# Sparse attention layer on one core: the rows of q tiles 10 and 11 go over DRAM into quarter order and are turned by VectorE instead of TensorE; two W_v transfers are issued later

## The chip, the cores and the metric

The kernel runs on one core of a Trainium2 chip. A core has five engines with a queue each: TensorE (PE; its weight loads are shown apart as PEld), VectorE (DVE), ScalarE (ACT), GpSimd (POOL) and SyncE (SP, which only issues transfers). ACT and POOL issue transfers too; all of them share 16 DMA engines. The metric is the device time of one execution in microseconds (us), the median of several runs; lower is better.

## The reference

x is 2708 x 1024, adj a random 0/1 matrix of 2708 x 2708 with about 4 ones in a row.

```
h = max(layernorm(x), 0)
q = h @ W_q.T + b_q ;  k = h @ W_k.T + b_k ;  v = h @ W_v.T + b_v
z = (q @ k.T) / sqrt(1024) * adj ;  z = -10000 where z == 0
out = x + relu(softmax(z, axis=1) @ v)
```

Everything is fp32.

## The kernel before, in words

**The mathematics.** Only the few pairs (row, neighbour) with adj = 1 count. The kernel forms M = W_q.T W_k once, then q' = h M + b for each row, and a score is the product of a row of q' with the neighbour's row of h. The weighted sum u of neighbours' rows of h comes before the product with W_v. So there are two long matrix products: "q units", rows of h times M, and "o units", rows of u times W_v.

**Tiles and units.** Rows are put in an order by number of neighbours (first 8 tiles of 128 rows, `EARLY = 8`, then the others). A unit is a pair of tiles and does a 256 x 1024 by 1024 x 1024 product by Strassen's scheme with seven block products instead of eight. Units 0 to 9 are q units on tiles (0,1) to (18,19), units 10 to 18 are o units; a single tile of u comes at the end. Unit 5 holds tiles 10 and 11. `FIRST = 4` is the first unit whose rows are read along with the attention, `last_q = 9`.

**One unit on TensorE** (`multiply`, L1050, and `opened`, L1016): `opened(n)` does a11 M11 into bank X, copies X to bank Y (L1024, ACT), then s1 T0 into bank Z, and copies Z to p5 (L1029, ACT). `multiply(n)` then does s2 T1 into Y, copies Y to u2 (L1060), a12 M into X, s4 M into Z, s3 T2 into Y, then `between(n)`, which opens the next unit, and a22 T3 into Y. The calls `after(0)` to `after(6)` between these blocks hang everything else on places "(n, i)": the operands of the next unit, loads, steps of the attention. s1 to s4 are sums of the quarter blocks a11, a12, a21, a22 of the unit's rows, transposed.

**The transposes.** The product needs the rows with the 1024 columns on the partitions. `half_turned` (L410 to L416) does this on TensorE, four 128 x 128 transposes into a PSUM bank, and ACT copies the bank to SBUF (L718), or VectorE reads it (L722). A unit of two tiles needs 16 transposes. For most tiles of u another way is in use: ACT copies the 128 x 1024 tile with its 32-column pieces regrouped (L944), writes it to DRAM (L946), four transfers from SP (`by_quarters`, L695 to L701) read it back with groups of 32 rows and of 256 columns exchanged, and VectorE turns the 32 x 32 blocks (`faces`, L703, two instructions of 128 x 512 for a tile). `is_faced` (L708) tells `blocks` (L711), which way a row tile came.

**The rows of q units.** Tiles 0 to 7 are kept from the normalisation. From unit 4 on, GpSimd gathers rows of h (L612, `load_rows`, L1204) by a table in row order. At place (2, 5) GpSimd's hand-written order is: add tiles 8 and 9 to the sum of all rows `hsum` (`owe`, L291, four adds of 128 x 256 for a tile, L298), gather the rows of unit 4, add tiles 10, 6 and 7, gather the rows of unit 5. Row tiles share 7 buffers (`ROWS = 7`).

**The order of work.** Until unit 3 ACT and DVE follow the order of the program text; from unit 4 on only DVE does, and a planner places the instructions of the other engines by its own times. `tc.issue_after(i)` puts an instruction behind i on i's engine.

**Attention** (`attention`, L959): VectorE multiplies and sums rows gathered by GpSimd (L610) with q rows (L863, scores) and then sums them with weights (L923). `advance` doles out these steps in the places. They start at the end of unit 4, once the table of the first 8 tiles is read back on SP (`reload`, L634, L638; step "b0" at place (4, 4)) and the q rows of a tile are gathered. An o unit's rows must be finished by then; the last single tile is turned by one VectorE instruction into `T_alone` (L1334).

**W_v.** In the q units the buffer M holds W_q.T W_k. Its block M[0][1], called t1 here, is free once the derived blocks T are made; in the o units it must hold W_v's block (0,1) minus block (0,0). At place (7, 0) SP loads block (0,0) into it (L1274, 1 MB), ACT negates it in two pieces (L1280), and GpSimd issues a transfer that adds block (0,1) (L1281, place (7, 6)). It is first used at place (9, 3), by VectorE (L1285). GpSimd, SP and ACT run ahead of the places where nothing holds them.

Of the kernel before, what the change touches and what calls it, by code (L numbers as in the profile page):

```python
# [10 lines left out]
FT = mybir.dt.float32  # L11
# [54 lines left out]
def tile_preln_masked_attention(  # L66
# [45 lines left out]
    q_late = dram.tile([(BARE - EARLY) * P, D], FT, name="q_late")  # L112
    u_dram = dram.tile([FULL * P, D], FT, name="u_dram")
# [195 lines left out]
    def follow(steps):  # L309

        for step in steps.split():
# [15 lines left out]
            elif step[0] == "p":  # L327
                counted(first)
            elif step[0] == "c":
                counts(*halves[first])  # L330
            elif step[0] == "o":
                sorted_at.append(sort(*halves[first]))
            elif step[0] == "w":
                pooled.close()
                with tc.issue_after((behind if first < EARLY else products)[-1].ins):
                    entered.append(put(first, int(last[0]) + 1))
            elif step == "z":
                pooled.enter_context(tc.manual_schedule(engines={mybir.EngineType.Pool}))
                with tc.issue_after(entered[-1].ins):
                    reload(EARLY, NT)  # L340
            elif step[0] == "b":
                reload(*halves[first])
            elif step[0] == "g":
                squared(first)
            else:
                if step[0] == "e":
                    counted(first)
                if step[0] != "j":
                    found(first, *[range(int(o[0]), int(o[-1]) + 1) for o in only])
                if step[0] != "i":  # L350
                    listed(first)
# [343 lines left out]
    def by_quarters(dst, rows):  # L695

        faced.append(dst)
        for a in range(QUADS):
            cols = slice(a * D // QUADS, (a + 1) * D // QUADS)
            nc.sync.dma_start(dst[a * QP:(a + 1) * QP, :].rearrange("r (g j) -> r g j", g=QUADS),  # L700
                              rows[:, cols].rearrange("(g r) j -> r g j", r=QP))  # L701
# [61 lines left out]
    def natural_rows(n):  # L763
# [252 lines left out]
    def opened(n):  # L1016
# [15 lines left out]
    def between(n):  # L1032
# [3 lines left out]
        else:  # L1036
            opened(n + 1)
        if n == last_q - 1:
# [11 lines left out]
    def multiply(n, results, after):  # L1050
# [9 lines left out]
        nc.scalar.copy(u2, Y)  # L1060
# [23 lines left out]
    def q_results(ta, tb):  # L1084
# [136 lines left out]

    products = []
# [14 lines left out]
    for n, unit in enumerate(units):  # L1237
# [8 lines left out]
        if n in (last_q, last_q + 1):  # L1246
            share -= 2.3 / 7 * (n - last_q + 1)
        nxt = units[n + 1] if n + 1 < len(units) else None
# [4 lines left out]
        def after(i):  # L1253
# [18 lines left out]
            for at, place, src in (((-2, 0), t1, of_wv(0, 0)), ((0, 3), b21, of_wv(1, 0))):  # L1272
                if (n - last_q, i) == at:
                    nc.sync.dma_start(place, src)  # L1274
# [3 lines left out]
            if (n - last_q, i) == (-2, 6):  # L1278
                for h in range(2):
                    nc.scalar.activation(t1[:, 2 * h:2 * h + 2], t1[:, 2 * h:2 * h + 2], AF.Copy, scale=-1.0)  # L1280
                nc.gpsimd.dma_start(t1, of_wv(0, 1), accum_op=ALU.add)  # L1281
# [18 lines left out]
            elif (n, i) == (FIRST, 6):  # L1300
                advance(share)
# [21 lines left out]
            if (n, i) == (3, 4):  # L1323
                searched()
            if (n, i) == (3, 6):
# [254 lines left out]
```

## Time and profile before

| | us |
|---|---|
| median of 3 runs | 629.07 |
| the runs | 627.19, 629.07, 629.32 |
| the profiled execution's own time | 627.16 |
| its span, first to last instruction | 625.5 |

The profiled execution has 6068 instructions in its span. In the chain of waits of the profile one unit's seven block products are 56 matmul records; times in the timeline are microseconds from the start of the span. The place (n, i) of the code is not in the profile; it is found from the order of the block products: the rows of unit 5 are transposed at 216.94 and 221.24 us, and the last o unit ends near 609 us. In a row of a timeline the brackets at the end tell how long the engine had been idle before it and what released it. A row of a source line gives durations in ns as least/median/greatest.

### The profile page before, as it was taken

The page shows a single profiled execution, that of the slowest core. Times are in us where ns is not written, and L with a number is a line of the kernel's source. Part 1 is how long each engine was busy: PE and PEld are TensorE (multiplying, and loading weights), DVE is VectorE, ACT ScalarE, POOL GpSimd, SP SyncE. Part 2 cuts the span into 40 slices and gives each one's busy share as a digit, 9 for nine tenths or more (in the row PEclk, how much of TensorE's full clock was granted, in tenths as well). Part 3 has the DMA queues.
Part 4 walks back from the last instruction along what each step waited for, and adds up shares of the span by engine and source line. Part 5 has one row for each costly group of instructions (what it writes and reads, how often), then busy time and mean ns, then how long its engine had stood idle before and what let it go on. Part 6 is the DMA issues. An engine that isn't in the chain of part 4 may idle for free.

```text
span 625.5 us, 6068 instructions
## 1 busy us (share of the span) xinstructions
PE 618.3 (99%) x1571; PEld 309.9 (50%) x1571; DVE 525.7 (84%) x1024; ACT 291.0 (47%) x421; POOL 368.9 (59%) x394
## 2 busy tenths in 40 slices
PE   9999999999999999999999999999999999999996
PEld 5777776444444444454444444444444444444442
DVE  5999878987988947979898999998988899898541
ACT  3538976749777373434331532443442433432300
POOL 2638870786668577856655343577577657752331
PEclk9999999999999999999999999999999999999998
DMA  8998898687797559997696999999999999995571
GB/s 336 407 374 318 332 352 326 211 273 292 267 370 277 175 180 364 342 347 233 218 362 170 397 340 313 339 326 320 328 328 320 333 306 338 288 301 144 137 266 71
DMA packets 65808, 183.24 MB, mean 293 GB/s; under 512 B 10039, under 2 KB 20615, under 8 KB 65128
## 3 DMA queue, kind: packets, MB, share of 16 engines
q0 software_dynamic: 26656, 86.02, 43.7%
q1 hardware_dynamic: 32170, 72.06, 33.0%
q10 hardware_dynamic: 6942, 24.73, 10.1%
q8 instruction: 14, 0.23, 0.1%
q14 instruction: 26, 0.21, 0.1%
HBM read 147.23 MB, written 43.88 MB: 306 GB/s over the span
## 4 chain that ended last, share of the span: by engine, by line
PE 90%; DMA 3%; POOL 2%; ACT 2%; DVE 1%; issue 0%; POOLq 0%; ACTq 0%
PE ps L1011 42%; PE psy L1011 30%; PE ps_y L476 7%; PE ps_x L476 4%; PE ps_z L476 4%; PE pt L415 2%; POOL hsum L298 2%; DMA x<-in_x_dram 2%; ACT sized L368 1%; DMA wlow<-in_wq_dram 1%; DVE wlow L444 1%; DVE s L722 0%; ACT junk_x L246 0%; PE ps_h L1230 0%; PE ps_v L594 0%
## 5 line engine op out<-in xcount | busy, mean ns | idle before, releaser
L610 POOL DMA_INDIRECT g<-h_dram,tab x93 | 120.5, 1296 | 62.4 <-issue 19.4
L1011 PE MATMUL psy<-wlow,s 128*128 128x512 f32 x320 | 144.0, 593 | 0.2 <-ACT u L1060 0.2
L1011 PE MATMUL ps<-M,a 128*128 128x512 f32 x320 | 144.1, 593 | 0.1
L863 DVE SCALAR_TENSOR_TENSOR junk<-g,pq 128x1024 uint8<-128x1024 f32 x92 | 112.3, 1220 | 9.3 <-DMA g<-h_dram,tab 7.3
L1011 PE MATMUL ps<-M,s 128*128 128x512 f32 x240 | 107.9, 592 | 0.0
L1011 PEld LDWEIGHTS ps<-M,a 128*128 128x128 f32 x320 | 60.0, 190 | 72.6 <-issue 71.5
L1011 PEld LDWEIGHTS psy<-wlow,s 128*128 128x128 f32 x320 | 60.0, 190 | 72.5 <-issue 71.3
L923 DVE SCALAR_TENSOR_TENSOR u<-g,coef,u 128x1024 f32<-128x1024 f32 x70 | 89.8, 1282 | 7.2 <-ACT u L912 5.4
L389 DVE FIND_INDEX8 at<-ones,adj 128x8 uint32<-128x685 f32 (+1 forms) x88 | 74.4, 863 | 0.0
L1011 PEld LDWEIGHTS ps<-M,s 128*128 128x128 f32 x240 | 45.5, 190 | 57.2 <-issue 55.5
L1011 PE MATMUL psy<-wlow,a 128*128 128x512 f32 x160 | 71.9, 592 | 0.0
L368 ACT ACTIVATE sized<-adj 128x2708 uint8<-128x2708 f32 (+1 forms) x22 | 54.3, 2468 | 7.5 <-DMA adj<-in_adj_dram 6.2
L298 POOL TENSOR_TENSOR hsum<-hsum,x 128x256 f32<-128x256 f32 (+1 forms) x56 | 38.6, 725 | 24.9 <-DVE wlow L444 21.5
L1115 POOL DMA_INDIRECT y<-in_x_dram,tab x19 | 33.2, 1749 | 31.4 <-ACT y L1132 16.6
L1011 PEld LDWEIGHTS psy<-wlow,a 128*128 128x128 f32 x160 | 30.4, 190 | 38.3 <-issue 36.6
L808 POOL DMA_INDIRECT out_dram<-y,tab x21 | 27.9, 1329 | 15.8 <-issue 13.6
L1011 PE MATMUL ps<-wlow,s 128*128 128x512 f32 x80 | 36.0, 593 | 0.0
L944 ACT COPY v<-u 128x1024 f32<-128x1024 f32 x20 | 20.9, 1046 | 29.9 <-DVE u L923 27.6
L912 ACT ACTIVATE u<-g,coef 128x1024 f32<-128x1024 f32 x16 | 18.4, 1148 | 25.7 <-DVE coef L911 20.5
L626 POOL DMA_INDIRECT tab_dram<-tab,pos_i x22 | 21.6, 982 | 14.3 <-DVE pos_i L689 8.8
L276 ACT ACTIVATE x<-x,r 128x1024 f32<-128x1024 f32 (+1 forms) x22 | 25.9, 1235 | 6.9 <-POOL r L266 6.9
L760 ACT COPY ps<-bp_sb 128x512 f32<-128x512 f32 x42 | 24.6, 596 | 8.7 <-DVE y L1150 7.2
(253 smaller groups left out, 839.1 us busy)
## 6 DMA issues: line engine op xcount, KB each, us to landing
adj<-in_adj_dram SPq DMA_DIRECT2D x21, 1354.0 KB, 11.4
x<-in_x_dram SPq DMA_DIRECT2D x21, 512.0 KB, 7.7
h_dram<-x ACTq DMA_DIRECT2D x21, 512.0 KB, 7.9
u_dram<-v ACTq DMA_DIRECT2D x20, 512.0 KB, 8.2
or<-u_dram SPq DMA_DIRECT2D x80, 128.0 KB, 7.9
q_late<-q SPq DMA_DIRECT2D x12, 512.0 KB, 8.5
pq<-q_late POOLq DMA_DIRECT2D x12, 512.0 KB, 9.3
M<-in_wv_dram SPq DMA_DIRECT2D x3, 1024.0 KB
```

The costliest lines, as they stand in the source:

```text
L276: nc.scalar.activation(xs[i][:n], xs[i][:n], AF.Relu, bias=r[:n, 4, i:i + 1], scale=r[:n, 3, i:i + 1])
L298: small.append(nc.gpsimd.tensor_add(hsum[:n, cols], hsum[:n, cols], xt[:n, cols]))
L368: nc.scalar.activation(sized[:n], a[:n, :, :PW], AF.Abs, accum_out=total[:n, t:t + 1])
L389: nc.vector.max_index(at[:n, k - first_k, g, :], ones[:n, 0:8], a[:n, g, :])
L476: mm = nc.tensor.matmul(bank, a_tile(o + H * a[0], a[1], i), b(o), start=first and o == 0, stop=(o == H - 1), skip_group_check=True)
L610: return nc.gpsimd.indirect_dma_start(out=dst, out_offset=None, in_=src, in_offset=off, bounds_check=N - 1, oob_is_err=False)
L760: nc.scalar.copy(return_[h], row[:, h * NB:(h + 1) * NB])
L808: to = nc.gpsimd.indirect_dma_start(out=out, out_offset=bass.IndirectOffsetOnAxis(ap=ptab.bitcast(U32)[:n, t, SLOTS:SLOTS + 1], axis=0), i ...
L863: chained(lambda: nc.vector.scalar_tensor_tensor(junk, g_of[t][s], 1.0, tq[t], op0=ALU.mult, op1=ALU.mult, accum_out=zall[:, t, s:s + 1]))
L923: chained(lambda: nc.vector.scalar_tensor_tensor(u, g_of[t][s], coef[:, s:s + 1], u, op0=ALU.mult, op1=ALU.add))
L1011: mm = nc.tensor.matmul(bank, a[:, c, :], b[:, c, :], start=False, stop=(c == 3), skip_group_check=True)
L1115: return nc.gpsimd.indirect_dma_start(out=y[:n], out_offset=None, in_=x, in_offset=off, compute_op=ALU.add)
```

## The change

The rows of unit 5 (tiles 10 and 11) take the way that tiles of u take. Once unit 4 is opened, ACT copies each of the two gathered tiles with its columns regrouped and writes it to a new DRAM buffer (`send_round`); SP reads each back with four transfers (`come_round`); VectorE turns them, two instructions of 128 x 512 a tile, at place (4, 2), where both halves are now made. For that the gather of tiles 10 and 11 stands ahead of the adds of tiles 10, 6 and 7 to `hsum`, and the gather of unit 6's rows is called at place (3, 4). The table's read back "b0" moves from (4, 4) to (4, 0), behind the transfers of `come_round` on SP, and the store of q tile 8 stands behind it.

Block (0,0) of W_v is loaded at (7, 5), behind the newest store of q on SP, and the store of q tile 16 stands behind that load. The negation on ACT and the adding transfer on GpSimd move to (8, 1), behind the newest u2 copy and the newest gather of the attention.

```diff
@@ by_quarters takes the queue and returns its last transfer
-    def by_quarters(dst, rows):
+    def by_quarters(dst, rows, eng=nc.sync):
...
             elif step[0] == "b":
-                reload(*halves[first])
+                with tc.issue_after(came[-1].ins):
+                    tabbed.append(reload(*halves[first]))
...
-                (3, 1): "i21", (3, 3): "p21", (3, 4): "j21 c0", (3, 5): "g0", (3, 6): "w0-7 g1 g2 g3 g4", (4, 4): "b0"}
+                (3, 1): "i21", (3, 3): "p21", (3, 4): "j21 c0", (3, 5): "g0", (3, 6): "w0-7 g1 g2 g3 g4", (4, 0): "b0"}
...
         if n == FIRST:
             follow("o0")
+            send_round(ROUND[0])
...
+        if n == FIRST - 1:
+            come_round(ROUND[0], nc.sync)
...
-            (nc.scalar if t < 4 else nc.sync).dma_start(dst, q)
+            behind_it = early_wv if t == units[last_q - 1][1] else tabbed if t == EARLY else None
+            with tc.issue_after(behind_it[-1].ins) if behind_it else nullcontext():
+                stored.append((nc.scalar if t < 4 else nc.sync).dma_start(dst, q))
...
+    ROUND = range(FIRST + 1, FIRST + 1 + 1)
+    stored, copied_at, came, tabbed, early_wv = [], [], [], [], []
+
+    def in_quarters(v, u):
+        return nc.scalar.copy(v.rearrange("p (a c r) -> p c a r", a=QUADS, r=QP),
+                              u.rearrange("p (c a r) -> p c a r", a=QUADS, r=QP))
+
+    def round_row(n, k):
+        t = 2 * (n - ROUND[0]) + k
+        return r_dram[t * P:(t + 1) * P, :]
+
+    def send_round(n):
+
+        for k, xt in enumerate(rows_of[n]):
+            v = row_tile(f"way_{n}_{k}")
+            in_quarters(v, xt)
+            nc.scalar.dma_start(round_row(n, k), v)
+
+    def come_round(n, eng):
+
+        rows_of[n] = [row_tile(f"came_{n}_{k}") for k in range(2)]
+        for k, xt in enumerate(rows_of[n]):
+            came.append(by_quarters(xt, round_row(n, k), eng))
...
                 rows_of[FIRST] = load_rows(units[FIRST])
+                rows_of[FIRST + 1] = load_rows(units[FIRST + 1])
                 owe(10)
                 owe(6)
                 owe(7)
-                rows_of[FIRST + 1] = load_rows(units[FIRST + 1])
...
-            for at, place, src in (((-2, 0), t1, of_wv(0, 0)), ((0, 3), b21, of_wv(1, 0))):
-                if (n - last_q, i) == at:
-                    nc.sync.dma_start(place, src)
+            if (n - last_q, i) == (-2, 5):
+                with tc.issue_after(stored[-1].ins):
+                    early_wv.append(nc.sync.dma_start(t1, of_wv(0, 0)))
+            if (n - last_q, i) == (0, 3):
+                nc.sync.dma_start(b21, of_wv(1, 0))
...
-            if (n - last_q, i) == (-2, 6):
-                for h in range(2):
-                    nc.scalar.activation(t1[:, 2 * h:2 * h + 2], t1[:, 2 * h:2 * h + 2], AF.Copy, scale=-1.0)
-                nc.gpsimd.dma_start(t1, of_wv(0, 1), accum_op=ALU.add)
+            if (n - last_q, i) == (-1, 1):
+                with tc.issue_after(copied_at[-1].ins), tc.issue_after(gathered[-1].ins):
+                    for h in range(2):
+                        nc.scalar.activation(t1[:, 2 * h:2 * h + 2], t1[:, 2 * h:2 * h + 2], AF.Copy, scale=-1.0)
+                    nc.gpsimd.dma_start(t1, of_wv(0, 1), accum_op=ALU.add)
...
-                    with tc.issue_after(products[-1].ins) if n + 1 == FIRST else nullcontext():
+                    if n + 1 != ROUND[0]:
+                        with tc.issue_after(products[-1].ins) if n + 1 == FIRST else nullcontext():
+                            ops_of[n + 1][1]()
+                if i == (4 if n == 0 else 5 if turn else 2):
+                    if n + 1 == ROUND[0]:
                         ops_of[n + 1][1]()
-                if i == (4 if n == 0 else 5 if turn else 2):
                     ops_of[n + 1][2]()
...
                 searched()
+                rows_of[FIRST + 2] = load_rows(units[FIRST + 2])
```

More of the change, by code (lines that the diff above doesn't have):

```diff
@@ L699, in by_quarters @@
             cols = slice(a * D // QUADS, (a + 1) * D // QUADS)
-            nc.sync.dma_start(dst[a * QP:(a + 1) * QP, :].rearrange("r (g j) -> r g j", g=QUADS),
-                              rows[:, cols].rearrange("(g r) j -> r g j", r=QP))
+            last = eng.dma_start(dst[a * QP:(a + 1) * QP, :].rearrange("r (g j) -> r g j", g=QUADS),
+                                 rows[:, cols].rearrange("(g r) j -> r g j", r=QP))
+        return last
     def faces(dst, xt, lo, hi):
@@ L1059, in multiply @@
         u2 = small("u2")
-        nc.scalar.copy(u2, Y)
+        copied_at.append(nc.scalar.copy(u2, Y))
         after(2)
@@ L1247, in tile_preln_masked_attention @@
             share -= 2.3 / 7 * (n - last_q + 1)
+        if n > FIRST and n + 1 in ROUND:
+            share -= 0 / 7
         nxt = units[n + 1] if n + 1 < len(units) else None
@@ L1300, in after @@
             elif (n, i) == (FIRST, 6):
-                advance(share)
+                advance(1 * share)
             if nxt is not None:
```

1 line of the change is left out of this document (added).

## The prediction

> **What bounds the kernel now.** First the page, busy shares and the DMA slices; then TensorE's own waits; then the chain of waits in order of time.
>
> ```profile
> PE 618.3 (99%) x1571; PEld 309.9 (50%) x1571; DVE 525.7 (84%) x1024; ACT 291.0 (47%) x421; POOL 368.9 (59%) x394
> ```
> ```profile
> DMA  8998898687797559997696999999999999995571
> ```
> ```profile
> PE ps_y L511 <- POOL hsum L121: 1.2, 1, 1.2
> PE ps_x L476 <- DMA wlow<-in_wq_dram: 0.2, 1, 0.2
> PE psy L1011 <- ACT u L1060: 0.2, 1, 0.2
> ```
> ```profile
> 216.94 0.87 PE pt L415 x8
> 217.81 3.44 PE psy L1011 x8
> 221.24 0.87 PE pt L415 x8
> ```
>
> TensorE is busy 99% of the span, and all its waits together are 1.6 us, 1.4 of them before its products begin. In the chain, eight matmul records of 512 columns take 3.44 us, eight transposes 0.87 us, and one piece begins where the last ended. So a cut in TensorE's work shows in full as long as nothing else comes late, and between its first and last product nothing outside TensorE can give more than those waits. The two transposing pieces at 216.94 and 221.24 are the rows of tiles 10 and 11. The change takes them away.
>
> ```profile
> L415 PE MATMUL pt<-ident,qr 128*128 128x128 f32 x96 | 12.4, 273 | 0.0
> ```
>
> **What is removed.** Of these 96 the 16 of one unit, 2 x 0.87 = 1.74 us of TensorE, and three ACT copies out of PSUM. This is the whole gain; every other edit can only cost.
>
> A page weighs this otherwise. The Trainium skill, page "VectorE: DVE Perf Modes", section "The three transpose paths", gives 390 ns for one 128 x 128 transpose on TensorE (bf16), and its rules advise TensorE for it where PSUM will do. Its figure would make the gain 16 x 0.39 = 6.2 us, an estimate from that page; its advice speaks against the move. In this trace a pipelined transpose takes 0.87/8 = 0.11 us, so I keep 1.74.
>
> **The way over DRAM: is it in time?** Unit 5's first product sets the clock:
>
> ```profile
> 232.42 6.87 PE ps L1011 x16
> ```
>
> After the change it stands at 232.42 - 1.74 = 230.7: a11 is due then, s1 3.4 us later, at 234.1. The rows in the order in which they are used: ACT's timeline, the lines of the copy, of the reading back and of the turns (least/median/greatest, ns), the DMA issues (KB, us to landing), VectorE's timeline, and the windows (PE, PEld, DVE, ACT, POOL busy, clock, DMA share, GB/s).
>
> ```profile
> 209.93 0.57 ACT L1024 COPY psy<-ps 128x512 f32<-128x512 f32 x1 [1.06 <-PE ps L1011]
> 213.54 0.58 ACT L1029 COPY p<-ps 128x512 f32<-128x512 f32 x1 [3.04 <-PE ps L1011]
> ```
> ```profile
> L944 ACT COPY v<-u x20: 1044/1046/1050, 249.1 to 586.5; 128x1024 f32<-128x1024 f32 x20
> ```
> ```profile
> L700 SPq DMA_DIRECT2D or<-u_dram x80: 302/431/1187, 321.2 to 592.3; - x80
> ...
> DMA to landing us min/median/max: 3.1/7.9/15.6
> ```
> ```profile
> L705 DVE STREAM_TRANSPOSE a<-or x29: 660/704/708, 347.3 to 573.6; 128x512 f32<-128x512 f32 x29
> ```
> ```profile
> u_dram<-v ACTq DMA_DIRECT2D x20, 512.0 KB, 8.2
> ```
> ```profile
> q_dram<-q SPq DMA_DIRECT2D x4, 512.0 KB, 3.7
> ```
> ```profile
> 221.43 0.91 DVE L1270 MEMSET g<- 128x1024 f32 x1 [0.16 <-issue]
> ```
> ```profile
> 229.03 0.69 DVE L1100 TENSOR_TENSOR q<-ps,u 128x512 f32<-128x512 f32 x1 [2.67 <-PE ps L1011]
> ```
> ```profile
> 200.00:216.00 16.00, 16.00 (x52) 7.92 (x52) 13.46 (x40) 6.86 (x11) 9.07 (x12) 1.00 0.48 166
> 216.00:226.00 10.00, 10.00 (x37) 5.36 (x36) 7.70 (x10) 9.03 (x17) 8.17 (x16) 1.00 0.19 61
> 226.00:240.00 14.00, 14.00 (x34) 6.11 (x34) 3.59 (x8) 5.31 (x10) 10.25 (x14) 1.00 0.93 319
> 300.00:310.00 10.00, 10.00 (x24) 4.37 (x23) 9.37 (x13) 3.37 (x6) 6.22 (x4) 1.00 0.61 205
> 310.00:335.00 25.00, 25.00 (x72) 11.95 (x71) 21.33 (x33) 8.24 (x15) 10.31 (x9) 1.00 0.79 269
> ```
>
> (1) ACT: the regrouping copies stand between the copies at 209.93 and 213.54, where ACT was idle 3.04 us. 210.5 + 2 x 1.05 = 212.6: 0.9 us are left, and the copies cost nothing; without that gap they would push the copy p, which is not needed for another 10 us (s4's product follows s2's and a12's). (2) The two stores, issued at 211.6 and 212.6, land after 3.7 us (the q stores, in calmer time) to 8.2 us (the same store later, under full DMA): at 215.3 and 216.3, or at 219.8 and 220.8. (3) SP issues eight transfers at 0.43 us: the last four from 217.0 to 218.7, or from 221.5 to 223.2. They land 3.1 to 7.9 us later, so the second tile is there between 221.8 and 231.1. I take the early end: DMA was at 0.48 and 0.19 of its time here, against 0.93 in the next stretch. (4) VectorE is at its memsets until 221.43 + 0.91 = 222.3; then four turns of 0.70 and four sums of 0.69, as long as the add at 229.03, make 5.6 us. By the early end a11 is ready at 223.0 and the last sum at 227.9, beside the add's 229.03 - 1.74 = 227.3, which no product waits for at once. By the late end the first tile's rows land at 229.4: a11 at 230.1 and a12 at 230.8; then a22 and a21 until 232.5 and s1 at 233.2. That is still in time, by 0.6 us for a11 and 0.9 us for s1. So TensorE loses nothing by either end; only the worst landing of that line, 15.6 us, brings a stall (rival D).
>
> What queues behind: on SP the store of q tile 7 and the table's read back, in GpSimd's queue three tiles of hsum behind two gathers.
>
> ```profile
> 225.16 0.38 SPq L638 DMA_DIRECT2D tab<-tab_dram  x1
> ```
>
> The read back waits for the table's writes and was issued at 225.16; the eight transfers are issued by 223.2 at the latest, so it loses nothing. The GpSimd work is the same in sum; I give it 0.
>
> Against the turns stands a rule of the Trainium skill, page "SBUF — State Buffer", section "SBUF: two separate sides": while VectorE holds the port pair that it shares with GpSimd, GpSimd can't write the descriptors of its transfers. The page doesn't say whether a turn holds that pair; what it would do here is rival C.
>
> **The W_v transfers.** The load in its old place on SP, the wait for it on ACT, the adding transfer, and on VectorE the add before the store that the load is now behind, the first score, and the line of t1's first use:
>
> ```profile
> 226.28 0.52 SPq L1274 DMA_DIRECT2D M<-in_wv_dram  x1
> ```
> ```profile
> 231.71 2.00 ACT L1280 ACTIVATE M<-M 128x1024 f32<-128x1024 f32 x2 [3.45 <-DMA M<-in_wv_dram]
> ```
> ```profile
> M<-in_wv_dram POOLq DMA_DIRECT2D x1, 1024.0 KB, 12.0
> ```
> ```profile
> 308.86 0.68 DVE L1100 TENSOR_TENSOR q<-ps,u 128x512 f32<-128x512 f32 x1
> ```
> ```profile
> 238.31 1.23 DVE L863 SCALAR_TENSOR_TENSOR junk<-g,pq 128x1024 uint8<-128x1024 f32 x1 [3.18 <-DMA g<-h_dram,tab]
> ```
> ```profile
> L1285 DVE TENSOR_TENSOR wlow<-wlow,M x2: 2283/2284/2284, 359.0 to 371.3; 128x2048 f32<-128x2048 f32 x2
> ```
>
> The load goes from 226.28 to behind the store of q tile 14, whose add ended at 308.86 + 0.68 = 309.5: issue near 309.5 - 1.7 = 308. It took 231.71 - 226.28 = 5.4 us; 12.0 is the row of the adding transfer. So it lands at 313 to 320, ACT negates for 2.0, and the adding transfer ends at 327 to 334. It is due at 359.0 - 1.7: over 20 us spare, no cost. On the DMA engines 2 MB move into 308 to 335. At 269/0.79 = 340 GB/s they take 6.2 us, and the two later windows have 0.39 x 10 + 0.21 x 25 = 9 us free: it fits. In its old place the load's 1 MB took 3.3 us at 319 GB/s, ahead of the first gathers. The first score, which waited for its gather until 238.31, can begin up to 3.3 us earlier; this gives VectorE slack, not TensorE time. At the new place ACT waits for the load with copies for TensorE behind it, and GpSimd for the negation with gathers behind it. I take 0 for both, for the old place cost TensorE nothing either, and carry the ends to the rivals.
>
> **The sum.** The profiled execution took 627.16 us (span 625.5). 627.16 - 1.74 + 0 = 625.4, a factor of 0.9972. That execution stands at the low end of the runs; against their median of 629.07 the forecast is 629.07 x 0.9972 = 627.3 us.
>
> **The rivals.**
>
> *A, the last tile takes the gain back.*
>
> ```profile
> 598.20 1.25 DVE L705 STREAM_TRANSPOSE T_alone<-or 128x1024 f32<-128x1024 f32 x1 [10.62 <-DMA or<-u_dram]
> ```
> ```profile
> 602.52 3.43 PE ps L1011 x8
> ```
>
> T_alone is ready at 599.45, after 10.62 us of waiting for its rows; TensorE uses it at 602.52, after the change at 600.8. That leaves 1.3 us. If VectorE's attention ends later by more than that, each microsecond is paid in full, and 3.0 us leave the time where it is: 627.2, median 629.1. For it: VectorE is 21.33 of 25 us busy in the last window above, and GpSimd's wait for the negation (0 to 7 us, by the landing) holds up gathers. Against it: the attention begins up to 3.3 us earlier, and the transfers fit.
>
> *B, slower: ACT stands before the negation.*
>
> ```profile
> 313.25 0.57 ACT L1024 COPY psy<-ps 128x512 f32<-128x512 f32 x1 [1.59 <-PE ps L1011]
> ```
> ```profile
> 320.95 3.44 PE psy L1011 x8
> ```
>
> If the planner puts the two negations ahead of the copy psy of unit 8 (313.25, after the change 311.5), ACT waits there for the 1 MB. TensorE needs that copy at 320.95 - 1.74 = 319.2. The load must land by 319.2 - 0.6 - 2.0 = 316.6, 8.6 us after its issue; from there each microsecond is one of TensorE. By the 12.0 us row it is 3.4 us: 627.16 - 1.74 + 3.4 = 628.8, median 630.7. For it: ACT did wait 3.45 us for this load. Against it: the load took 5.4 us there, at a DMA share of 0.93.
>
> *C, GpSimd is locked out by the turns.* Four turns, 2.8 us, hold up the table's writes and so the first gathers; with A's 1.3 us TensorE would lose 1.5 at the end: 626.9, median 628.8. Against it:
>
> ```profile
> 347.31 1.29 DVE L705 STREAM_TRANSPOSE a<-or 128x512 f32<-128x512 f32 x2
> ```
> ```profile
> 347.41 0.99 POOL L610 DMA_INDIRECT g<-h_dram,tab  x1 [0.30 <-DVE junk L863]
> ```
>
> A gather issued amid two turns took 0.99 us and did not wait for their end at 348.6. By that rule, if it covers turns, it would have; the trace disagrees.
>
> *D, the rows of unit 5 land late.* With 15.6 us from 223.2 they are there at 238.8 and s1 at 240.9, 6.8 us late: 632.2, median 634.1. Against it: the idle DMA of that stretch. That the rows stay on TensorE, the change doing nothing, would be 629.1; the diff marks them as faced, so I give it next to nothing.
>
> **How the numbers follow.** Chances: forecast 0.70, A 0.12, B 0.07, C 0.03, D 0.03, and 0.05 for a little more than 1.74, as the 0.2 us wait of mid-kernel and a shorter end could add (2.3: median 626.8). The runs stand in two groups 2 us apart (627.19, and 629.07 with 629.32), so the median after may be one of the lower group: 627.19 x 0.9972 = 625.4. Half a per cent, about what a measurement of this kernel can tell from no change, is 3.1 us: the bounds are 625.9 and 632.2. Faster needs the forecast or more (0.75) and the lower group (0.27): 0.20. Slower needs D, or B beyond its 12.0 us: 0.07. Within: 0.73. The range goes from 624.9 (lower group, 0.5 us more gained) to 630.6 (B), which leaves out D and a gain of over 2.3.
>
> **What would show it.** Right: 80 instead of 96 transposes pt<-ident,qr; unit 5 opened near 230.7; four turns on VectorE from 222.3; PE's waits still under 2 us; the last product 1.7 us earlier. Wrong: a wait of PE on ACT between 311 and 320 (B), on VectorE near 600 (A) or 230 (D), or writes of the table over 1 us long beside the turns (C). The forecast is wrong if PE's waits grow by over a microsecond, or if the planner reorders ACT or SP elsewhere so that a bank comes late.

## The result, and the profile after

The changed kernel takes 633.04 us (median of seven runs, 631.37 to 636.86), the kernel before beside it 627.6 us: ratio 1.0083, 95% interval 1.0059 to 1.0107. It is slower by 5.4 us, and the forecast of 627.3 us and its range up to 630.6 us both missed. The profiled execution took 633.04 us (span 631.3).

The half of the change that goes over DRAM ran nearly to the time forecast. These are timelines of the kernel after (start, duration, instruction): ACT's copies and stores, SP's reading back, VectorE's turns; then the chain of waits.

```profile
210.55 1.05 ACT L1234 COPY way<-qr 128x1024 f32<-128x1024 f32 x1
211.63 0.33 ACTq L1246 DMA_DIRECT2D r_dram<-way  x1
```
```profile
214.55 3.88 SPq L702 DMA_DIRECT2D came<-r_dram  x8
```
```profile
221.94 1.83 DVE L708 STREAM_TRANSPOSE a<-came 128x512 f32<-128x512 f32 x3
223.70 0.67 DVE L708 STREAM_TRANSPOSE s<-came 128x512 f32<-128x512 f32 x1
```
```profile
213.64 6.87 PE psy L1014 x16
220.50 6.87 PE ps L1014 x16
...
230.81 6.87 PE ps L1014 x16
```

The transposes of unit 5 are gone from the chain, and the unit opens at 230.81 instead of 232.42. So TensorE was 1.6 us ahead. It was lost, and more, in TensorE's own waits, which stand a good 120 us later: the groups of PE's waits, and its timeline (in brackets the idle time before a product, and what ended it).

```profile
PE psy L1014 <- DVE q L1105: 3.0, 1, 3.0
PE ps_y L513 <- POOL hsum L122: 1.2, 1, 1.2
PE ps L1014 <- DVE s L745: 1.0, 1, 1.0
PE psy L1014 <- ACT u L1066: 0.6, 1, 0.6
```
```profile
352.66 3.60 PE L1014 MATMUL ps<-M,s 128*128 128x512 f32 x8
...
356.91 3.70 PE L1014 MATMUL psy<-wlow,s 128*128 128x512 f32 x8 [0.65 <-ACT u L1066]
361.63 3.67 PE L1014 MATMUL ps<-M,a 128*128 128x512 f32 x8 [1.02 <-DVE s L745]
365.14 3.60 PE L1014 MATMUL ps<-M,s 128*128 128x512 f32 x8
371.73 5.40 PE L1014 MATMUL psy<-wlow,a 128*128 128x512 f32 x8 [2.99 <-DVE q L1105]
376.96 3.60 PE L1014 MATMUL psy<-wlow,s 128*128 128x512 f32 x8
```

Between the starts at 352.66 and 376.96 lie five products. Without waits they take 5 x 3.43 = 17.2 us; here they took 24.3. So 7.1 us were lost within 25 us: 1.6 gained, 7.1 lost, 5.5 net. The three waits are 4.7 us of it. Another 1.8 us are in the product at 371.73, which took 5.40 us instead of 3.60 although the profile names no wait inside it: TensorE's granted clock fell to 0.50 right behind the longest stall (windows: length, busy time of PE, PEld, DVE, ACT and POOL, clock, DMA share, GB/s).

```profile
372.00:373.00 1.00, 1.00 (x3) 0.25 (x3) 1.00 (x3) 0.15 (x2) 0.00 (x0) 0.70 1.01 275
373.00:374.00 1.00, 1.00 (x3) 0.48 (x2) 1.00 (x1) 0.53 (x2) 0.00 (x0) 0.50 1.12 277
```

So part of the loss is not a wait, but comes behind one. The waits name three different releasers, so the reader must look for what stands behind all three. Most of it stands one step back, on ACT and on VectorE:

```profile
354.71 0.59 ACT L763 COPY ps<-bp_sb 128x512 f32<-128x512 f32 x1 [7.59 <-DMA bp_sb<-in_bv_dram]
355.24 1.14 ACT L906 ACTIVATE u<-hsum,m 128x1024 f32<-128x1024 f32 x1
356.29 0.57 ACT L1066 COPY u<-psy 128x512 f32<-128x512 f32 x1
```
```profile
354.66 0.69 DVE L1387 TENSOR_TENSOR bp_sb<-bp_sb 128x512 f32<-128x512 f32 x1 [6.10 <-DMA bp_sb<-in_bv_dram]
```
```profile
338.46 0.35 SPq L1385 DMA_DIRECT2D bp_sb<-in_bv_dram  x1
```

Both engines stand still for the row of v's bias, 512 KB issued at 338.46; VectorE goes on 16.2 us later. Behind the bank's copy on ACT queues u2's copy, for which TensorE waits first; behind the subtraction on VectorE queue the rows of the next unit and the sums q. Before the change the same row came in 10.5 us, and ACT waited 0.76 us:

```profile
340.24 0.38 SPq L1344 DMA_DIRECT2D bp_sb<-in_bv_dram  x1
```
```profile
350.79 0.59 ACT L760 COPY ps<-bp_sb 128x512 f32<-128x512 f32 x1 [0.76 <-DMA bp_sb<-in_bv_dram]
```
```profile
bp_sb<-in_bv_dram SPq DMA_DIRECT2D x1, 512.0 KB, 10.5
```

The row itself was not touched by the change. What did change is the work of the DMA engines in front of it. The windows (PE, PEld, DVE, ACT, POOL busy, clock, DMA share, GB/s), before and after:

```profile
320.00:330.00 10.00, 10.00 (x37) 5.41 (x36) 9.79 (x18) 4.30 (x8) 2.29 (x2) 1.00 0.94 305
330.00:335.00 5.00, 5.00 (x13) 2.13 (x13) 3.37 (x10) 1.61 (x3) 0.57 (x1) 1.00 0.19 40
335.00:340.00 5.00, 5.00 (x13) 2.25 (x12) 4.96 (x6) 0.81 (x2) 4.37 (x3) 1.00 0.65 209
340.00:345.00 5.00, 5.00 (x13) 2.25 (x12) 4.86 (x5) 1.16 (x2) 3.78 (x5) 1.00 1.01 282
```
```profile
320.00:330.00 10.00, 10.00 (x31) 4.90 (x30) 9.11 (x19) 5.78 (x12) 3.79 (x4) 1.00 0.98 281
330.00:335.00 5.00, 5.00 (x13) 2.20 (x12) 3.98 (x4) 1.29 (x2) 3.62 (x2) 1.00 1.08 198
335.00:340.00 5.00, 5.00 (x13) 2.28 (x12) 4.70 (x5) 0.57 (x1) 3.85 (x4) 1.00 1.03 321
```

Before, the DMA engines had worked off their backlog by 330, and there was a pause ahead of the row's issue at 340.24, with shares of 0.19 and 0.65. After, there is no pause: they go into the row's time full. The suspect is the late pair of W_v transfers, which the experiments test:

```profile
306.67 1.67 SPq L1308 DMA_DIRECT2D M<-in_wv_dram  x1
```
```profile
317.97 2.00 ACT L1317 ACTIVATE M<-M 128x1024 f32<-128x1024 f32 x2 [5.77 <-DMA M<-in_wv_dram]
```
```profile
320.28 0.99 POOL L1318 DMA_DIRECT2D M<-in_wv_dram  x1 [4.63 <-ACT M L1317]
```

A second transfer behind the row came late as well: the load of W_v's block (0,0) into M[0][0], the operand of the first product of unit 10, which starts at 361.63.

```profile
344.29 0.33 SPq L1046 DMA_DIRECT2D M<-in_wv_dram  x1
```

It landed 17.2 us after its issue, at 361.5. Without any stall its product would have stood at 352.66 + 2 x 3.43 = 359.5, 2 us earlier. In this execution VectorE's s ended at the same moment and is the releaser named.

### The profile page after: what moved, and what is told of

Its sections match the earlier page's. It is cut to its first block, busy times and chain, and to the rows that moved or that the text cites. A ratio compares the mean times of both kernels' runs of the same rounds, so it can differ in the third digit from the quotient of the medians.

```text
span 631.3 us, 6055 instructions
## 1 busy us (share of the span) xinstructions
PE 619.6 (98%) x1555; PEld 308.7 (49%) x1555; DVE 528.0 (84%) x1028; ACT 292.9 (46%) x420; POOL 370.0 (59%) x394
## 3 DMA queue, kind: packets, MB, share of 16 engines
q10 hardware_dynamic: 7230, 25.78, 10.5%
## 4 chain that ended last, share of the span: by engine, by line
PE 86%; DMA 9%; DVE 2%; issue 1%; ACT 1%; POOL 0%; SPq 0%; POOLq 0%; DVEq 0%; ACTq 0%
PE ps L1014 39%; PE psy L1014 28%; PE ps_y L478 7%; PE ps_x L478 4%; PE ps_z L478 4%; DMA or<-u_dram 3%; DMA bp_sb<-in_bv_dram 3%; DMA g<-h_dram,tab 2%; PE pt L417 2%; DMA M<-in_wv_dram 2%; PE ps_y L513 1%; DVE u L926 1%; DVE s L725 0%; DVE junk L866 0%; ACT M L1317 0%
## 5 line engine op out<-in xcount | busy, mean ns | idle before, releaser
L612 POOL DMA_INDIRECT g<-h_dram,tab x93 | 121.8, 1310 | 69.1 <-DVE u L926 30.5
L1014 PE MATMUL psy<-wlow,a 128*128 128x512 f32 x160 | 73.7, 604 | 3.0 <-DVE q L1105 3.0
L1123 POOL DMA_INDIRECT y<-in_x_dram,tab x19 | 33.4, 1757 | 32.8 <-ACT y L1140 18.3
L478 PE MATMUL ps_y<-wlow 128*128 128x512 f32 x64 | 27.6, 592 | 0.0
```

Source lines behind the costliest of these rows:

```text
L478: mm = nc.tensor.matmul(bank, a_tile(o + H * a[0], a[1], i), b(o), start=first and o == 0, stop=(o == H - 1), skip_group_check=True)
L612: return nc.gpsimd.indirect_dma_start(out=dst, out_offset=None, in_=src, in_offset=off, bounds_check=N - 1, oob_is_err=False)
L1014: mm = nc.tensor.matmul(bank, a[:, c, :], b[:, c, :], start=False, stop=(c == 3), skip_group_check=True)
L1123: return nc.gpsimd.indirect_dma_start(out=y[:n], out_offset=None, in_=x, in_offset=off, compute_op=ALU.add)
```

## The experiments

Kernels of one group ran on one chip beside the kernel before. Ratios are to that kernel.

| group | kernel | median us | before us | ratio | 95% interval |
|---|---|---|---|---|---|
| I | round_only | 626.2 | 627.55 | 0.9982 | 0.9969 to 0.9996 |
| I | wv_only | 632.18 | 627.55 | 1.0078 | 1.0054 to 1.0102 |
| I | no_wv | 626.62 | 627.55 | 0.9977 | 0.9964 to 0.9991 |
| I | no_add | 625.01 | 627.55 | 0.9958 | 0.9943 to 0.9972 |
| II | after_bias_act | 633.61 | 630.86 | 1.005 | 1.0027 to 1.0073 |
| II | round_bias_act | 631.73 | 630.86 | 1.002 | 1.0 to 1.004 |
| II | add_late | 631.87 | 630.86 | 1.0033 | 1.0008 to 1.0058 |
| II | plain | 635.74 | 630.86 | 1.0083 | 1.0057 to 1.0109 |
| III | mid_wv | 628.07 | 627.46 | 1.0007 | 0.9994 to 1.0019 |
| III | after_again | 631.87 | 627.46 | 1.0076 | 1.0058 to 1.0095 |
| III | plain_again | 627.54 | 627.46 | 1.0 | 0.9976 to 1.0024 |
| III | round_only_again | 626.51 | 627.46 | 0.9984 | 0.9968 to 1.0 |
| IV | no_bias | 628.31 | 627.32 | 1.0016 | 1.0001 to 1.0031 |
| IV | dummy | 629.49 | 627.32 | 1.0034 | 1.0014 to 1.0055 |
| IV | after_third | 632.26 | 627.32 | 1.0074 | 1.0053 to 1.0094 |
| IV | plain_third | 629.73 | 627.32 | 1.0038 | 1.0011 to 1.0064 |

**Group I: each half alone, and the two transfers left out.** The kernel round_only undoes the W_v edits (its code, shortened):

```
-            if (n - last_q, i) == (-2, 5):
-                with tc.issue_after(stored[-1].ins):
-                    early_wv.append(nc.sync.dma_start(t1, of_wv(0, 0)))
...
+            for at, place, src in (((-2, 0), t1, of_wv(0, 0)), ((0, 3), b21, of_wv(1, 0))):
+                if (n - last_q, i) == at:
+                    nc.sync.dma_start(place, src)
...
+            if (n - last_q, i) == (-2, 6):
...
+                nc.gpsimd.dma_start(t1, of_wv(0, 1), accum_op=ALU.add)
```

> The changed kernel with the W_v edits undone: block (0,0) of W_v is loaded, negated and added to at the places of before; the way of tiles 10 and 11 over DRAM stays. Theory W (the late W_v transfers fill the DMA engines ahead of the load of the bias row, L1385 of the changed kernel; its landing went from 10.5 to 16.2 us and ACT and VectorE waited 7.6 and 6.1 us for it): the stall between 354 and 372 us is gone, ACT waits under 1 us for the bias row, ratio to before 0.997 (627.6 - 1.75 = 625.9). Theory R (the way over DRAM itself, by its order or its transfers): still slow, ratio 1.005 to 1.010. Theory E (the attention begins earlier because the load is not in front of its first gathers, and its gathers now meet the bias row): fast as well, since the load is back in front.

The other half, wv_only, puts the two late transfers into the kernel before.

> The kernel before with the W_v edits alone: the load behind the store of q tile 14, the negation and the adding transfer at (8, 1); q rows 10 and 11 are turned by TensorE as before. Theory W: slow, by the 6.6 us of stalls of the changed kernel without its gain of 1.75: ratio 1.007 to 1.012, ACT waits 5 us or more for the bias row. Theory E: slow in the same way, since the attention begins earlier here too. Theory R: no change, 0.998 to 1.002.

Two kernels take work out of the changed kernel: no_wv the load, the negation and the adding transfer of the block, no_add the adding transfer alone (the line that it leaves out):

```
-                    nc.gpsimd.dma_start(t1, of_wv(0, 1), accum_op=ALU.add)
```

> The changed kernel without the three W_v steps on M's block (0,1): no load of block (0,0) into it, no negation, no adding transfer; the o units then multiply with a block of the wrong matrix. The attention begins as early as in the changed kernel. Theory W: the bias row lands in 8 to 11 us, no stall near 354, ratio 0.997 or a little less. Theory E: slow as the changed kernel, ratio 1.005 to 1.010, since its gathers run just as early. Theory R: slow too.

> The changed kernel without the adding transfer alone; load and negation stay where the change put them, and the block then holds only minus block (0,0) of W_v. Theory W with the adding transfer as the bulk (it moves 1 MB in 12.4 us, while the DMA engines are full at only 150 to 180 GB/s): bias row in 11 to 12 us, ratio 0.997 to 0.999. Theory W with the load as the bulk: bias row still over 14 us, ratio over 1.003. Theories E and R: slow as the changed kernel.

The way over DRAM alone is faster, 0.9982; the W_v edits alone give nearly the whole loss, 1.0078. In round_only the load was back at 225.86, but the planner put the adding transfer at 298.29 (257.99 before), not at its old time. In wv_only the DMA queue's row, and ACT's and PE's waits, read as in the changed kernel:

```profile
338.26 0.38 SPq L1351 DMA_DIRECT2D bp_sb<-in_bv_dram  x1
```
```profile
ACT ps L760 <- DMA bp_sb<-in_bv_dram: 7.4, 1, 7.4
```
```profile
PE psy L1011 <- DVE q L1099: 2.8, 1, 2.8
PE ps L1011 <- DMA M<-in_wv_dram: 1.2, 1, 1.2
```

With no_wv attention starts nearly as early as in the changed kernel (first score at 237.14, against 236.55 there and 238.31 before), and nothing is lost: an earlier start is not the cause. In its profiled execution ACT still waits 2.9 us for the row and TensorE 1.5 us for q; its ratio is 0.9977 all the same. With no_add, where the late load and the negation stay and ACT waits 7.7 us for the load, the ratio is the lowest of all, below the 0.997 to 0.999 that were expected; its windows have the pause again, if a short one:

```profile
330.00:335.00 5.00, 5.00 (x13) 2.28 (x12) 3.67 (x8) 1.95 (x3) 3.02 (x3) 1.00 0.49 137
335.00:340.00 5.00, 5.00 (x13) 2.20 (x12) 4.90 (x5) 0.57 (x1) 4.09 (x4) 1.00 0.94 266
```

So it is the late W_v traffic, and without its last megabyte the loss is gone altogether. A rival is not excluded by these two kernels: GpSimd's wait of 4.63 us for the negation, with gathers behind it, goes away in both. Two later kernels bear on it. add_late has no such wait, and its DMA engines are full up to 340 all the same; the profiled execution of plain_third has one of 4.32 us, and TensorE loses 0.5 us. So that wait is neither needed for the full engines nor enough for the loss; how much it adds is not shown.

**Group II: the bias row from another queue, the adding transfer alone, a plain transfer.** If the late row were all, issuing it earlier would repair the kernel. Two kernels issue it from ACT, behind the last copy of q's bias, one on the changed kernel and one on the way over DRAM alone:

```
-                nc.sync.dma_start(bp_sb, bv.to_broadcast([P, D]))
+                nc.scalar.dma_start(bp_sb, bv.to_broadcast([P, D]))
```

> The changed kernel with one line moved to another queue: the bias row's load is issued by ACT, behind the last copy of the bias into a bank in the last unit but two, instead of by SP. Theory W (the bias row's load comes late, and ACT and VectorE stand before it): the load is issued near 331 instead of 338.5, while the adding transfer is still under way, and lands 10 to 17 us later, by 348; ACT and VectorE wait at most 1 us for it, PE's wait for q on VectorE falls from 3.0 to at most 1.5 us, the last tile's first product stands near 602 instead of 608, ratio to the kernel before 0.996 to 0.999. Rival V (the full DMA engines delay the gathers, and VectorE's attention is late whatever the bias row does): the bias row is there in time, but PE still waits 2 to 3 us for q, ratio above 1.004.

> The way over DRAM alone, W_v transfers as before, and the bias row's load issued by ACT. Both theories: the DMA engines are half free here between 330 and 340, so the load lands soon after its issue near 331, ACT's 0.8 us wait for it goes to 0, and PE's wait of 1.0 us for q on VectorE goes or stays. By W the ratio is 0.9955 to 0.998, at best 1 us below the way over DRAM alone (0.9982); if the bias row has no part in it, 0.998 as without the edit.

The edit did not do what was expected of it: ACT reached the issue at 338.1, no earlier than SP had. In after_bias_act nobody waited for the row all the same (ACT first used it at 353.4), and still the ratio was 1.005, where 0.996 to 0.999 was expected. TensorE lost time at the first product of unit 10 (PE's timeline, and SP's load of block (0,0)):

```profile
366.94 5.37 PE L1014 MATMUL ps<-M,a 128*128 128x512 f32 x8 [2.42 <-DVE m L902]
```
```profile
348.60 0.35 SPq L1046 DMA_DIRECT2D M<-in_wv_dram  x1
```

VectorE's m has nothing to do with that product; its operand, block (0,0), was issued 18.3 us before. That it waited for this block is argued here; the next groups name the wait. The round_bias_act kernel missed its expectation: 1.002, not below 0.998. All four kernels of this group wait 1.8 to 2.2 us for a gather of qr, which in the other groups only dummy does (0.7 us). The chip differs, its executions scatter more (628.35 to 634.66 us for the kernel before), and the changed kernel was not timed on it. So nothing is concluded from this group's ratios by themselves.

Next, add_late: the way over DRAM, load and negation at their old places, and only the adding transfer late.

> The way over DRAM, with the load of W_v and its negation at their old places (near 226 and 231), and only the adding transfer at its new, late place on GpSimd. Theory W-add (the adding transfer alone fills the DMA engines ahead of the bias row): the share is above 0.9 from 320 to 335 and the bias row takes over 13 us to land, ACT waits 3 to 7 us for it, PE waits over 2 us for q, ratio 1.004 to 1.009. Rival W-sum (only the two transfers together, 2 MB, are too much): the transfer is issued 5 us earlier as nothing waits for the negation, the engines are free again by 335, the bias row lands within 12.5 us, ratio 0.997 to 1.000.

It came out between the two: the DMA share is 1.01, 0.98 and 1.03 in the three windows from 320 to 340, as expected of the adding transfer alone, but ACT waits 1.4 us for the row, PE 1.7 us for q, and the ratio is 1.0033. One late megabyte, issued at 321.4, brings part of the loss here; but no_add, whose one late megabyte is the load, has none.

The kernel plain replaces the adding transfer by a plain load of the same bytes.

```
-                    nc.gpsimd.dma_start(t1, of_wv(0, 1), accum_op=ALU.add)
+                    nc.gpsimd.dma_start(t1, of_wv(0, 1))
```

> The changed kernel, but the adding transfer is a plain load of the same 1 MB from the same block on the same queue (the sum of the two blocks is left out). Theory W-kind (an adding transfer holds the DMA engines for longer than its bytes): the load lands in 4 to 9 us instead of 12.4, the rate in the full stretch is 300 GB/s or more, the share falls below 0.7 somewhere between 330 and 340, the bias row lands within 13 us, PE waits at most 1.5 us for q, ratio 0.996 to 0.999. Rival W-bytes (what counts is the 2 MB): as the changed kernel, 16 us, ratio 1.006 to 1.010.

The ratio, 1.0083, lies where W-bytes put it. Its profiled execution, 628.79 us, was the fastest of its eleven and shows no such loss, and the changed kernel did not run beside it; it was tried again in the next groups.

**Group III: the place of the transfers.** The kernel mid_wv has the two transfers one unit earlier than the change, but still later than before:

```
-            behind_it = early_wv if t == units[last_q - 1][1] else tabbed if t == EARLY else None
+            behind_it = early_wv if t == units[last_q - 2][1] else tabbed if t == EARLY else None
...
-            if (n - last_q, i) == (-2, 5):
+            if (n - last_q, i) == (-3, 5):
...
-            if (n - last_q, i) == (-1, 1):
+            if (n - last_q, i) == (-2, 1):
```

> The changed kernel with its two W_v transfers one unit of products (24 us) earlier: the load behind the store of q tile 12 instead of 14 (issue near 283), negation and adding transfer one unit earlier too (issue near 296). They are still 40 to 55 us later than in the kernel before. Theory W2 (what was used up is the pause of the DMA engines from 328 to 340, in which the backlog of gathers is worked off before the bias row and the W_v blocks, which are due within 7 to 15 us): now the pause is there again, the share falls below 0.75 somewhere between 328 and 340, the bias row lands within 13 us, PE waits at most 1.5 us for q and nothing for M, ratio 0.996 to 1.000 (0.997 to 0.999 likeliest). Rival L (any place later than the old one costs, since the DMA engines are full from 240 on and the attention falls behind by the same 2 MB): PE loses 2 us or more at 355 to 375 or at the last tile, ratio above 1.004.

> The changed kernel once more, as the measure for the other kernels of this call on the same chip. By every theory a ratio of 1.006 to 1.011; and if the place of the loss wanders with the chip's DMA (the bias row first in one profile, the block b21 of W_v in the run with the bias row on ACT's queue), PE's waits between 354 and 377 sum to 3 to 7 us, on whatever they fall.

> The way over DRAM alone, W_v transfers at their old places, on the chip of this call. If its gain of 1.1 us (0.9982) is that of the 16 transposes and not of one chip: 0.996 to 0.999 again. If it rests on the chip: 1.000 to 1.003, as the same kernel with the bias row on ACT's queue had it elsewhere.

> The changed kernel with a plain load in place of the adding transfer (the sum of the two blocks is left out), beside the changed kernel on the same chip. W-kind (an adding transfer holds the DMA engines for longer than its bytes): at least 2 us faster than the changed kernel in this call. W-bytes (what counts is the 2 MB in 307 to 335): within 1 us of it. The profile of the earlier run was its fastest execution, and tells less than its median, which stood at 1.0083.

The load was issued at 282.8 and the adding transfer at 299.27, and the pause is back:

```profile
330.00:335.00 5.00, 5.00 (x13) 2.15 (x12) 3.37 (x11) 1.42 (x3) 0.57 (x1) 1.00 0.42 84
335.00:340.00 5.00, 5.00 (x13) 2.28 (x12) 4.96 (x6) 1.49 (x3) 4.18 (x3) 1.00 0.60 194
```

Nobody waits for the row, PE's waits for q are 0.9 us, and 3.8 us of the changed kernel's 631.87 are gone; the ratio, 1.0007, is just above the 0.996 to 1.000 that were expected. The rest, 1.6 us above round_only_again, is not explained by its profile. That the adding transfer may be late as such is seen in the two round_only kernels: it stood at 298.3 and 298.7 in them, some 22 us ahead of the changed kernel's, and nothing was lost. In after_again the changed kernel's loss shows the second carrier, a transfer that brings the loss to TensorE, named directly:

```profile
PE psy L1014 <- DVE q L1105: 2.7, 1, 2.7
PE ps L1014 <- DMA M<-in_wv_dram: 1.3, 1, 1.3
```

Several loads go into M. The one that this wait is for is block (0,0), L1046: it landed 17.7 us after its issue at 344.41, at 362.1, and its product began at 362.23. The expectations of this and the next group name another block, b21 (L1310, issued 352.77); nothing waited for that one, and it is first multiplied in the fourth product of unit 10, at 379.01 here. Block (0,0) took 17.2, 17.7 and 18.0 us in the three profiles of the changed kernel, and 13.8 to 15.0 in no_add, mid_wv and both round_only kernels.

**Group IV: who carries the loss to TensorE.** The kernel no_bias leaves the row's load out; dummy moves its 512 KB into the scratch rows r_dram instead, behind SP's newest read back, where nobody waits for them (the edit of dummy):

```
-                nc.sync.dma_start(bp_sb, bv.to_broadcast([P, D]))
+                with tc.issue_after(quartered[-1].ins):
+                    nc.sync.dma_start(r_dram[0:P, :], bv.to_broadcast([P, D]))
```

> The changed kernel without the load of v's bias row (left out: the banks of the last units start from q's bias row instead of v's). Theory B (TensorE's loss is the wait of ACT and VectorE for this row and what queues behind it): the waits for the row go, PE's wait for q falls to 1 us or less, ratio 0.996 to 0.999. Theory W2 (the engines are still full at 340, and with the row gone the W_v block b21, due 7 us after its place comes free, and the gathers are late in its stead): PE waits 2 to 4 us for M or for q at 355 to 375, ratio 1.002 to 1.006. By both it can't be slower than the changed kernel in this call.

> As the kernel without the bias row's load, but the same 512 KB are still moved at the same place of SP's queue, into the scratch rows in DRAM, where nobody waits for them (v's bias row is left out as there). Theory B: nobody waits, so as that kernel, ratio 0.996 to 1.000. Theory W2 (the bytes hold up b21 and the gathers as well): 1 to 3 us slower than that kernel, ratio 1.004 to 1.009, PE's waits between 354 and 377 at 3 us or more.

> The changed kernel, as the measure for the other kernels of this call on the same chip: ratio 1.006 to 1.011, PE's waits between 354 and 377 of 4 to 7 us.

> The changed kernel with a plain load in place of the adding transfer (the sum of the two blocks is left out), beside the changed kernel on the same chip. W-kind (the adding transfer holds the DMA engines for longer than its bytes): 2 to 5 us below the changed kernel of this call, as on the chip before. W-bytes: within 1 us of it. In between, or in two groups: the bytes alone bring the stage to the edge, and the kind pushes it over in every execution.

Without the row 4.0 us of after_third's 632.26 are gone, with its bytes but without the waits 2.8. So the row carries most of the loss, and neither theory holds alone: of the changed kernel's 1.0074, 0.0016 stay without the row and 0.0034 with its bytes. How the row's part divides into the wait and the bytes is less sure. The intervals of no_bias and dummy overlap, and those of dummy and after_third overlap slightly; and in its profiled execution dummy issued the bytes at 341.81, 4.5 us later than after_third its row, and block (0,0) behind them 4.5 us later too. The profiled execution of no_bias, its fastest, shows no loss. That of dummy, the longest of its runs with 633.37 us, lost time in one place, though nobody waits for a bias row there:

```profile
365.83 5.08 PE L1016 MATMUL ps<-M,a 128*128 128x512 f32 x8 [4.54 <-DMA M<-in_wv_dram]
```
```profile
347.80 0.35 SPq L1048 DMA_DIRECT2D M<-in_wv_dram  x1
```

This load is block (0,0) again. It landed 17.9 us after its issue, at 365.7; its product was due at 357.69 + 3.43 = 361.1. Behind the wait this product, too, ran at a lower granted clock, 0.50 from 366 to 368.

Whether the adding kind or the bytes count: in both groups the plain load is faster than the changed kernel, by 4.3 us (III) and 2.5 us (IV, where the two intervals overlap slightly). But its executions lie far apart, from 625.2 to 632.6 and from 625.9 to 634.4, where the changed kernel's lie between 630.4 and 634.4. The DMA views of a stretch around the transfer, changed kernel (320 to 334) and plain_third (319 to 335):

```profile
M<-in_wv_dram POOLq DMA_DIRECT2D x1, 1024.0 KB, 12.4
```
```profile
M<-in_wv_dram POOLq DMA_DIRECT2D x1, 1024.0 KB, 9.4
```

The plain load of plain_again took 9.5 us, the adding transfer at this late place 10.6 to 12.4 in wv_only, dummy, no_bias and the three profiled executions of the changed kernel. So with the bytes alone the stage is at its edge, where some executions lose and some don't; with the adding kind all twelve executions of the changed kernel in these two groups took 630.4 us or more. That the 1 to 3 us which the adding transfer takes longer are the reason is likely, but rests on one profile of each run.

Of all kernels here that compute the whole result, round_only is the fastest, and faster than both given ones: 0.9982 and 0.9984 on two chips.

## Why the prediction was wrong

**The gain, 2 x 0.87 us: right.** The group of transposes in the page after has 80 of them, and TensorE was 1.6 us ahead at unit 5 and still at 282:

```profile
L417 PE MATMUL pt<-ident,qr 128*128 128x128 f32 x80 | 10.4, 273 | 0.0
```

Where nothing else comes late it reaches the end: round_only has 1.0 to 1.4 us of it in the median, while no_add has 2.5, 0.8 more than was removed, which no run explains.

**The way over DRAM, cost 0: right, by the early end that was taken.** ACT's copies started at 210.55 (forecast 210.5), SP's eight transfers were out by 218.4 (218.7), the turns began at 221.94 (222.3), the unit opened at 230.81 (230.7).

**The W_v transfers, cost 0: wrong, and this is the step that failed.** The term put at 0 was 4.6 us by itself (wv_only against the kernel before) and 5.4 us beside the way over DRAM (after_again against round_only_again). The prediction had the load at 308, the adding transfer's end at 327 to 334, and both held (306.67; 320.28 + 12.4 = 332.7). What failed is the sentence "it fits" and the conclusion "over 20 us spare, no cost". Two errors are in it. First, the free share was averaged over 310 to 335 and priced at 340 GB/s; the full engines moved 281 GB/s in 320 to 330 and 198 in 330 to 335, and they stayed full past 340. Second, the due time asked for was that of the moved transfer, t1, which indeed was never late. The due times that mattered were those of the transfers behind it: the bias row and block (0,0) for M[0][0]. The row's thin margin could have been read before the change: ACT's wait of 0.76 us for it, and the 0.19 share ahead of it, in a window that the average of 0.79 over 25 us had hidden. What the prediction also left out is what follows a stall: 1.8 of the 7.1 us were lost to the lower clock behind it.

**Rival A did not come about:** T_alone's wait for its rows was 10.26 us after and 10.62 before, and the loss had been made by 377. **Rival B was half seen:** ACT did wait for the load, 5.77 us until 317.97, but behind the copy psy (311.63), not ahead of it; only the copy p was late, at 319.88, and no product waited for it. **Rival C was not seen:** the table's writes took 984 ns on average after, 982 before. The rule of the Trainium skill on the port pair (page "SBUF — State Buffer", section "SBUF: two separate sides") is, if it covers turns, not confirmed by this trace. **Rival D was not seen:** all turns were over by 224.4. The sign that the prediction gave for being wrong was seen: PE's waits grew from 1.6 to 5.8 us. The loss is a rival that the list lacked; its nearest relative was the last sentence of the prediction, "a bank comes late".

What stays open: how the 5 us are shared between the carriers in any one execution (dummy, against after_third, gives 2.8 us to the wait for the row, with the doubts named there; the rest is its bytes, block (0,0) and the clock), the 1.6 us of mid_wv, and why the gain was not seen in group II.

## What to carry to other kernels

A transfer that is moved costs the DMA engines its time at the new place even where its own due date is far: look at the windows of a few microseconds right ahead of the next transfers with a due date, and reckon that those transfers may need a pause there as their slack. A wait of under a microsecond on a DMA, harmless before, says how near that edge is. Where a stall names several releasers, go back one step on the queue of each; they may have waited for the same transfer. Where several loads go into one buffer, find out by the landing times of each line which of them a wait was for.

## What the runs showed of the hardware

Full DMA engines moved anything between 198 and 424 GB/s in windows of 5 us of the changed kernel, so that neither share nor rate alone tells what fits. The packets differ (two windows of the changed kernel, 330 to 335 and 350 to 355):

```profile
DMA packets 563, 0.99 MB, mean 198 GB/s; under 512 B 91, under 2 KB 401, under 8 KB 561
```
```profile
DMA packets 504, 2.12 MB, mean 424 GB/s; under 512 B 100, under 2 KB 113, under 8 KB 381
```

Both had a share of over 1.0 and about as many packets; in the slow one 401 of 563 were under 2 KB, in the other 113 of 504. The adding transfer, too, was under way in the slow one, until 332.7; no run separates the two.

An adding transfer of 1 MB took 10.6 to 12.4 us where a plain one at the same place took 9.4 and 9.5; it took 8.3 us in mid_wv, next to a stretch in which the engines were 0.60 busy, but 10.6 and 10.5 us in the two round_only kernels, where it was issued within a microsecond of that time.

TensorE's granted clock fell to 0.50 right behind a stall of TensorE in five kept profiles (after, after_third, dummy, plain_again, after_bias_act; stalls of 2.6 to 4.7 us, from the starts of the products), and the next product took 1.5 to 1.8 us longer. In after_again and wv_only, behind stalls of 2.9 and 3.0 us, it stayed at 1.00. So the length of the stall does not decide it alone, and what does is not shown.
